# Mixture-of-experts blocks whose weighted results are added to each token's row in DRAM by accumulating scatters

## The chip, the cores and the metric

One core of one Trainium2 chip runs the whole program. The metric is the device time of one execution in microseconds (us), lower is better. Three runs of the kernel before gave 983.85, 988.71 and 992.39 us; their median is 988.71 us. The profile shows one further execution of 982.89 us, whose instructions span 980.9 us.

## What is computed

Four decoder layers work on `x` of 4 x 256 tokens with 256 features (1,024 tokens, eight tiles of 128). Each layer adds a gated attention and a gated feed-forward part to `x`. The change touches the feed-forward parts of layer 0 and layer 3, both mixtures of experts. Layer 0, cut to what matters:

```python
probs = softmax(xf @ gate_w.T)
_, idx = top_k(probs + gate_b, 6)            # 6 of 16 experts per token
cw = weights of the chosen experts, 0 elsewhere    # [tokens, 16]
def expert_step(y, params):
    W1, B1, W2, B2, W3, B3, c = params
    h = silu(xf @ W1.T + B1) * (xf @ W3.T + B3)    # 176 wide
    return y + c[:, None] * (h @ W2.T + B2)
z = shared expert of width 352 with its own biases
x = x + tanh(g_ffn[0]) * (y + z)
```

Layer 3 does the same with 8 experts of width 512, two per token with weights that are divided by their sum, no biases, and a shared expert of width 512. Its result is the program's output.

## The kernel before

**Routing.** `ffn0` and `ffn3` normalise `x` tile by tile. `stored` writes the normalised tokens to a DRAM tensor `xd`, one row of 1 KB per token. The generator `chosen` computes the router's weights `cw`, and `placed` sorts the (token, choice) pairs into blocks of 128 places, each block belonging to one expert: it leaves index columns `gather` and `scatter`, the expert of each block, and `weight`, one number per token and choice. These steps are mostly VectorE instructions; they are handed out one by one between the shared expert's steps `up`, `turn`, `down` (layer 0: L1295 to L1328), which add the shared expert to `x[t]` with `gated_add` (L424).

**Blocks.** `Experts.blocks` (L1225) runs a pipeline over 55 blocks in layer 0 and 20 in layer 3. In step i it gathers the rows of block i+4 (`fetch`, an indirect DMA issued by GpSimd, L1129), transposes block i (`turn`), turns the hidden values of block i-2 (`turn_hidden`), multiplies block i-1 by its expert's first weights (`up`), and block i-2 by the second (`down`). `down` copies the 128 result rows to one of eight places of `ring` and sends them with a second indirect DMA from GpSimd (L1205) to `z`, a DRAM tensor with one row for every (choice, token) pair: 6,144 rows in layer 0, 2,048 in layer 3. No two places share a row, and the scatters are declared independent of each other. Places that hold no token carry an index beyond the end and are skipped. More blocks stand under a condition (L1222) that was false in the profiled run: every engine reads the count and branches past them.

Between layer 0's blocks the generator `fold1` prepares layer 1's weights on TensorE, `ternary1` quantises others on VectorE, and `between` builds 32 diagonal matrices from the weights (L1358).

**Combining.** `combine` (L1241) is called for each of the eight token tiles after all scatters. It loads the tile's rows of `z` with SyncE's queue (L1250; 768 KB per tile in layer 0, in two loads), and adds them with their weights: in layer 0 four of six choices by a matmul with the diagonal matrices into PSUM (L1260), two on VectorE (L1263), and the experts' output biases by a transpose of `cw[:, t, :]` and a matmul with `b2_0` (L1367 to L1370); L1267 then adds PSUM to `x[t]`. In layer 3 both choices go over VectorE. After layer 0, the loads of layer 3's first four experts (L265) wait for the last of these additions, and layer 1's attention starts with `normalised()` on `x` (L354 to L376) and its first matmuls (L389). After layer 3, eight DMAs store `x` (L1619).

Each engine takes its instructions in order. DMAs of one issuing engine are issued in order; SyncE carries all plain loads and stores here, GpSimd all indirect ones.

Of the kernel before, what the change touches and what calls it, by code (L numbers as in the profile page):

```python
# [37 lines left out]
P = 128  # L38
# [19 lines left out]
PEK = 4  # L58
# [18 lines left out]
NOWHERE = 16384.0  # L77
C_SLOTS = 3
FIXED = 2 * DC + 8 + 2 * E0 + E0 + 8 + 2 * E3 + 4 + 1 + NB0 + 8 + 1 + L + 2
FIXED16 = P + K0 * NT + P + E0 * E0  # L80
# [3 lines left out]
def tile_flamingo(ctx: ExitStack, tc: tile.TileContext, a: dict, out: bass.AP):  # L84
# [98 lines left out]
    shared_32 = take(2)[:96]  # L183
    place = take(P, left16)
    tile_of = take(K0 * NT, left16)
# [115 lines left out]
    def prepare():  # L301
# [40 lines left out]
        for rows in (slice(32, 64), slice(64, 96), slice(64, 96)):  # L342

            nc.vector.tensor_tensor(bias_t[rows], bias_t[rows], bias_0[rows], ALU.subtract)
            nc.vector.tensor_copy(bias_0[rows], bias_t[rows])
            yield

# [568 lines left out]
    def chosen(xT, w, n, keep, bias, gate, extra, cut):  # L916
# [45 lines left out]
        nc.vector.tensor_scalar(cw, cw, gate, None, ALU.mult)  # L962
        yield
        return cw, mask

    def placed(cw, mask, n, keep, nb, stride, cut, keeping):
# [66 lines left out]
        for k in range(keep):  # L1033
# [16 lines left out]
                v[:, :, 1, :], is_in, tile_of[:, ts].unsqueeze(2).to_broadcast([P, NT, nb]), ALU.mult  # L1050
# [17 lines left out]
        nc.vector.tensor_scalar(none, row, 0.0, NOWHERE, ALU.is_equal, ALU.mult)  # L1068
# [17 lines left out]
        yield  # L1086
        weight = keeping([P, keep, NT])
        for k in range(keep):
            nc.vector.scalar_tensor_tensor(
                own[:, k, :].rearrange("p (t e) -> p t e", e=n), rank, float(k + 1), cw[:, :, :n], ALU.is_equal, ALU.mult  # L1090
            )
        nc.vector.tensor_reduce(
            weight.rearrange("p k t -> p (k t)"), own.rearrange("p k (t e) -> p (k t) e", e=n), AX.X, ALU.add
        )
        return gather, scatter, expert, offset, weight, used_blocks

    def finish_of(gen, out):

        out.append((yield from gen))

    def stored(normal, name):

        xd = dram.tile([T, D], F32, tag=name, name=name)
        for g, xn in enumerate(normal):
            for i, n in enumerate(xn):
                t = g * TPG + i
                nc.sync.dma_start(out=xd[t * P : (t + 1) * P, :], in_=n)
        return xd

    class Experts:  # L1110


        def __init__(self, route, xd, keep, nb, stride, width, chunk, group, w, bias, hTs, between):
            self.gather, self.scatter, self.expert, self.offset, self.weight, self.used = route
            self.xd, self.keep, self.nb, self.stride = xd, keep, nb, stride
            self.width, self.chunk, self.n = width, chunk, width // chunk
            self.group, self.w, self.bias, self.hTs = group, w, bias, hTs
            self.z = dram.tile([keep * T, D], F32, tag=f"z{group}", name=f"z{group}")
            self.between = between
            self.ring = [sb.tile([P, 4, D], F32, tag="xT", name="ring", bufs=2) for _ in range(2)]  # L1120
            self.scatters: list = []
# [4 lines left out]
        def fetch(self, b):  # L1126

            xs = sb.tile([P, D], F32, tag="xn", name="xs", bufs=6)
# [8 lines left out]
        def turn(self, b):  # L1137
# [4 lines left out]
            del self.xs[b]  # L1142
            nc.vector.tensor_copy(st[:, :D], ps[:, :D])  # L1143
            self.st[b] = st
# [4 lines left out]
        def up(self, b):  # L1149
# [28 lines left out]
            nc.vector.tensor_tensor(s, lin, s, ALU.mult)  # L1178
# [10 lines left out]
        def down(self, b):  # L1189
# [13 lines left out]
            else:  # L1203
                nc.scalar.copy(y, ps[:, :D])
            s = nc.gpsimd.indirect_dma_start(  # L1205
                out=self.z,
# [3 lines left out]
                bounds_check=self.keep * T - 1,  # L1210
                oob_is_err=False,
            )
            if self.scatters:
                tc.declare_no_dep(s.ins, group=self.group, reason="no two places share a row")
            tc.add_to_no_dep_group(self.group, s.ins)
            self.scatters.append(s)
# [24 lines left out]
        def combine(self, t, chunk, diag, more=None):  # L1241


            rows = self.z.rearrange("(k t p) d -> t p k d", t=NT, p=P)
            ps = ps_mm()[:, :D]
            started = more(ps) if more else False
            ends = max(diag, default=-1)
            for lo in range(0, self.keep, chunk):
                zt = t4([P, chunk, D], "zt")
                ld = nc.sync.dma_start(out=zt, in_=rows[t][:, lo : lo + chunk, :])  # L1250
                for s in self.scatters:
                    tc.add_manual_dep(
                        ld.ins,
                        s.ins.name,
                        mybir.DependencyInfo(mybir.DependencyClass.Sync, mybir.DependencyReason.DATA),
                        reason="any place may hold any row",
                    )
                for k in range(lo, lo + chunk):
                    if k in diag:
                        nc.tensor.matmul(ps, diag[k], zt[:, k - lo, :], start=not started, stop=(k == ends))  # L1260
                        started = True
                    else:
                        nc.vector.scalar_tensor_tensor(  # L1263
                            x[t], zt[:, k - lo, :], self.weight[:, k, t : t + 1], x[t], ALU.mult, ALU.add
                        )
# [112 lines left out]
    def ffn3(gate):  # L1378
# [57 lines left out]
        for t in range(NT):  # L1436
            moe.combine(t, K3, {})
# [317 lines left out]
```

## Time and profile before

| what | value |
|---|---|
| median of three runs | 988.71 us |
| profiled execution, its span | 982.89 us, 980.9 us |
| TensorE busy, its mean clock | 872.9 us (89%), 0.939 |
| VectorE, ScalarE, GpSimd busy | 531.6, 274.3, 300.0 us |
| layer 0: first gather, first and last scatter issued | 268.57, 282.32, 446.72 us |
| layer 0: first and last load of `z` | 452.12 us; all 16 issued over 19.4 us |
| layer 3: first and last scatter issued | 857.21, 963.87 us |
| layer 3: loads of `z` begin, stores of `x` begin | 966.46, 971.59 us |
| gather, scatter on GpSimd, each | about 0.97 and 1.02 us |

The columns of a timeline line are start, duration, engine, source line, operation, what it writes and reads, count, and in brackets the idle time of the engine before it with the engine that ended it. A `q` behind an engine's name means its sequencer, as for DMAs that it issues. An indirect DMA's duration on GpSimd is that of its issue; its data land later. Only waits on the engine that is late cost time, so the stages have to be read one by one.

### The profile page before, as it was taken

The numbers are of one execution on the slowest core, as the hardware profiler recorded it, in microseconds if no ns is written. First come the engines' busy times: TensorE is split into PE (matmuls) and PEld (weight loads), VectorE is DVE, ScalarE is ACT, GpSimd is POOL, SyncE is SP. The second block draws the span as 40 slices with busy tenths as digits, with TensorE's granted clock in tenths as the row PEclk, the third lists the DMA queues.
The fourth block names the chain that finished last, engine by engine and source line by source line (L and its number), as shares of the span: only waits on it lengthen the run. The fifth ranks groups of instructions, "written<-read, shape, count | busy, mean of one in ns | idle before, by whom it ended". The sixth has DMA issues, their size and how long they took to land.

```text
span 980.9 us, 12657 instructions
## 1 busy us (share of the span) xinstructions
PE 872.9 (89%) x4451; PEld 569.9 (58%) x4453; DVE 531.6 (54%) x1185; ACT 274.3 (28%) x531; POOL 300.0 (31%) x259
## 2 busy tenths in 40 slices
PE   5999998999899999997899978979638899999992
PEld 3544335876678866774547854746424556666661
DVE  4656455756953344552627749958785855222213
ACT  2211013334123232331223447034303532122220
POOL 1445451310065665751003128003101402133220
PEclk9999999999989999997999999979858989999997
DMA  9200017300154444225730000530000011011004
GB/s 351 84 15 11 28 36 230 89 22 22 33 153 160 131 152 151 90 69 157 260 115 1 1 1 27 189 116 2 22 0 1 1 44 33 22 48 39 29 16 140
DMA packets 35481, 75.82 MB, mean 77 GB/s; under 512 B 4551, under 2 KB 22207, under 8 KB 34106
## 3 DMA queue, kind: packets, MB, share of 16 engines
q1 hardware_dynamic: 27834, 56.22, 17.1%
q0 software_dynamic: 7296, 18.50, 6.1%
q8 instruction: 39, 0.64, 0.3%
q10 hardware_dynamic: 288, 0.26, 0.1%
q14 instruction: 24, 0.20, 0.1%
HBM read 63.42 MB, written 12.98 MB: 78 GB/s over the span
## 4 chain that ended last, share of the span: by engine, by line
PE 53%; DVE 17%; issue 14%; DMA 8%; POOL 4%; ACT 4%; SPq 0%; POOLq 0%; DVEq 0%; ACTq 0%
PE wide L389 9%; PE wide L1158 5%; PE mm L624 5%; DMA zz<-ring,scratch 4%; PE mm L1193 3%; PE wide L1400 3%; PE mm L419 2%; PE mm L1532 2%; POOL zz L1205 2%; PE mm L389 2%; PE wide L609 2%; PE mm L685 1%; PE mm L1421 1%; PE mm L897 1%; PE mm L671 1%
## 5 line engine op out<-in xcount | busy, mean ns | idle before, releaser
L405 POOL TENSOR_TENSOR attn<-attn,sm 128x1024 f32<-128x1024 f32 x32 | 60.8, 1900 | 235.1 <-DVE sm L404 163.1
L1178 DVE TENSOR_TENSOR blk<-wide,blk 128x176 f32<-128x176 f32 (+1 forms) x75 | 32.5, 433 | 142.0 <-ACT blk L1177 142.0
L650 DVE TENSOR_TENSOR rope<-wide,big 128x512 f32<-128x512 f32 x96 | 59.6, 683 | 57.1 <-PE wide L389 55.6
L389 PE MATMUL wide<-xT,big 128*128 128x512 f32 x192 | 88.8, 610 | 0.3 <-ACT big L524 0.3
L1129 POOL DMA_INDIRECT xs<-xd,big x55 | 55.3, 1005 | 70.3 <-DVE shared L1310 34.5
L1158 PE MATMUL wide<-big,blk 128*128 x220 | 74.1, 458 | 0.0
L1169 PE MATMUL wide<-big,blk 128*128 x160 | 72.2, 593 | 0.5 <-DVE blk L1143 0.5
L1205 POOL DMA_INDIRECT zz<-ring,big x55 | 56.1, 1021 | 31.9 <-DVE ring L1202 11.2
L389 PEld LDWEIGHTS wide<-xT,big 128*128 128x128 f32 x192 | 35.7, 193 | 48.7 <-issue 38.7
L1177 ACT ACTIVATE blk<-wide 128x176 f32<-128x176 f32 (+1 forms) x75 | 29.4, 392 | 122.8 <-PE wide L1158 61.6
L624 PE MATMUL mm<-vo,attnT 128*128 128x256 f32 x256 | 60.4, 390 | 0.9 <-ACT attnT L420 0.9
L1193 PE MATMUL mm<-big,blk 88*128 x220 | 56.8, 379 | 0.5 <-ACT blk L1186 0.5
L624 PEld LDWEIGHTS mm<-vo,attnT 128*128 128x128 f32 x256 | 48.4, 194 | 9.5 <-ACT attnT L420 3.3
L420 ACT COPY attnT<-mm 128x512 f32<-128x512 f32 x64 | 35.0, 588 | 65.0 <-PE mm L419 65.0
L374 PE MATMUL mm<-ident,xn 128*128 128x128 f32 x112 | 24.3, 363 | 30.3 <-DVE xn L362 18.0
L1193 PEld LDWEIGHTS mm<-big,blk 88*128 88x128 f32 x220 | 41.4, 189 | 15.5 <-ACT blk L1186 1.4
L1158 PEld LDWEIGHTS wide<-big,blk 128*128 128x128 f32 x220 | 39.5, 190 | 12.5
L403 DVE TENSOR_REDUCE sm<-attn 128x16 f32<-128x1024 f32 x32 | 38.9, 1215 | 14.5 <-ACT attn L397 12.3
L419 PE MATMUL mm<-ident,attn 128*128 128x128 f32 x256 | 36.3, 289 | 10.8 <-POOL attn L405 10.8
L1169 PEld LDWEIGHTS wide<-big,blk 128*128 128x128 f32 x160 | 28.8, 190 | 28.9 <-issue 28.2
L424 DVE SCALAR_TENSOR_TENSOR x<-mm,tg,x 128x256 f32<-128x256 f32 x48 | 22.9, 476 | 39.8 <-PE mm L624 19.7
L1129 POOL DMA_INDIRECT xs<-xd,scratch x20 | 19.2, 961 | 81.5 <-PE mm L1141 59.5
(334 smaller groups left out, 1702.4 us busy)
## 6 DMA issues: line engine op xcount, KB each, us to landing
big<-in_L_w_gate_up SPq DMA_DIRECT2D x8, 1024.0 KB, 8.2
zt<-zz SPq DMA_DIRECT2D x16, 384.0 KB, 5.1
big<-in_L_w SPq DMA_DIRECT2D x4, 1408.0 KB, 6.8
big<-in_L_w_down SPq DMA_DIRECT2D x8, 512.0 KB, 11.9
w_L_qk<-in_L_qk SPq DMA_DIRECT2D x4, 896.0 KB, 8.6
big<-in_L_w SPq DMA_DIRECT2D x4, 704.0 KB
big<-in_L_wo SPq DMA_DIRECT2D x1, 2048.0 KB, 12.8
xd<-xn SPq DMA_DIRECT2D x16, 128.0 KB, 1.8
```

Source lines behind the costliest of these rows:

```text
L389: nc.tensor.matmul(ps, w(c), xT[:, c, :], start=(c == 0), stop=(c == 1))
L403: nc.vector.tensor_reduce(sm, e, AX.X, ALU.add)
L405: nc.gpsimd.tensor_tensor(e, e, sm.unsqueeze(2).to_broadcast([P, groups, n]), ALU.mult)
L419: nc.tensor.transpose(ps[:, i * P : (i + 1) * P], ev[:, pr * P : (pr + 1) * P], ident)
L420: nc.scalar.copy(aT[:, half * 4 : half * 4 + 4, :].rearrange("p i t -> p (i t)"), ps)
L624: nc.tensor.matmul(ps[:, :D], aT[:, s, :], vo[:, s, :], start=(s == 0), stop=(s == NP - 1))
L650: nc.vector.tensor_tensor(m[:, s, :].rearrange("q (b t) -> q b t", t=S), ps[:, s, :].rearrange("q (b t) -> q b t", t=S), table, ALU.mult,)
L1129: nc.gpsimd.indirect_dma_start(out=xs, out_offset=None, in_=self.xd, in_offset=bass.IndirectOffsetOnAxis(ap=self.gather[:, b : b + 1].bitc ...
L1158: nc.tensor.matmul(ps[:, 0, : 2 * n], st[:, c * P : (c + 1) * P], self.w[:, bass.ds(r + c * 2 * n, 2 * n)], start=False, stop=(c == 1),)
L1169: nc.tensor.matmul(ps[:, k, :n], st[:, c * P : (c + 1) * P], self.w[:, bass.ds(r + (2 * c + k) * n, n)], start=(c == 0), stop=(c == 1),)
L1193: nc.tensor.matmul(ps[:, :D], hT[:, j * P : (j + 1) * P], self.w[: self.chunk, bass.ds(r + j * D, D)], start=(j == 0), stop=(j == self.n - 1),
L1205: s = nc.gpsimd.indirect_dma_start(out=self.z, out_offset=bass.IndirectOffsetOnAxis(ap=self.scatter[:, b : b + 1].bitcast(U32), axis=0), i ...
```

## The change

Each block's hidden values are multiplied by the token's weight, which now travels with the token: `xd` rows get 16 (layer 3: 8) more columns with all weights of the token, and each block picks its expert's column. The results are added by the scatter itself (`compute_op=ALU.add`) to the token's own row of a DRAM tensor, `sums0` in two copies for layer 0 (blocks alternate), `sums3` in one for layer 3. The first copy is filled with `x` after the shared expert (`keep_rows`), the second with zeros early in the program. Unused places add to spare rows. `combine`, `z`, the diagonal matrices and `weight` go. The scatters are no longer declared independent, so those that write the same tensor wait for each other. After layer 0 the first copy is loaded into `x` and the second added; after layer 3 `sums3` is copied to the output by DMA. The matmul with the output biases moves into the shared expert's `down`.

```diff
+    spare = take(1)
...
+        zeros = t4([P, 1024], "zeros")
+        nc.gpsimd.memset(zeros, 0.0)
+        for half in range(2):
+            zeroed(sums0[1][half * TH : (half + 1) * TH], zeros)
+        for sums in (*sums0, *sums3):
+            zeroed(sums[T:], zeros)
+        yield
+    sums0 = [dram.tile([T + P, D], F32, tag=f"sums0{i}", name=f"sums0{i}") for i in range(2)]
+    sums3 = [dram.tile([T + P, D], F32, tag="sums3", name="sums3")]
+    def zeroed(rows, zeros):
+        nc.sync.dma_start(out=rows.rearrange("(p r) d -> p (r d)", p=P), in_=zeros[:, : rows.shape[0] * D // P])
+    def keep_rows(sums):
+        for t in range(NT):
+            nc.sync.dma_start(out=sums[t * P : (t + 1) * P, :], in_=x[t])
...
-        weight = keeping([P, keep, NT])
-        for k in range(keep):
-            nc.vector.scalar_tensor_tensor(
-                own[:, k, :].rearrange("p (t e) -> p t e", e=n), rank, float(k + 1), cw[:, :, :n], ALU.is_equal, ALU.mult
-            )
-        nc.vector.tensor_reduce(
-            weight.rearrange("p k t -> p (k t)"), own.rearrange("p k (t e) -> p (k t) e", e=n), AX.X, ALU.add
-        )
...
-        xd = dram.tile([T, D], F32, tag=name, name=name)
+        xd = dram.tile([T, D + n], F32, tag=name, name=name)
...
+    def with_weights(xd, gated):
+        nc.sync.dma_start(out=xd[:, D:].rearrange("(t p) e -> p t e", p=P), in_=gated)
@@ Experts.turn(b)
+            n = self.experts
+            own = small([P, E0], "own")
+            w = self.weight[b] = small([P, 1], "weight", 4)
+            nc.vector.scalar_tensor_tensor(
+                own[:, :n],
+                block[:, :n],
+                self.expert[:, b : b + 1],
+                self.xs.pop(b)[:, D:],
+                ALU.is_equal,
+                ALU.mult,
+                accum_out=w,
+            )
...
-            nc.vector.tensor_tensor(s, lin, s, ALU.mult)
+            nc.vector.scalar_tensor_tensor(s, lin, self.weight.pop(b), s, ALU.mult, ALU.mult)
...
-            s = nc.gpsimd.indirect_dma_start(
-                out=self.z,
+            nc.gpsimd.indirect_dma_start(
+                out=self.sums[b % len(self.sums)],
                 out_offset=bass.IndirectOffsetOnAxis(ap=self.scatter[:, b : b + 1].bitcast(U32), axis=0),
                 in_=y,
                 in_offset=None,
-                bounds_check=self.keep * T - 1,
-                oob_is_err=False,
+                compute_op=ALU.add,
             )
-            if self.scatters:
-                tc.declare_no_dep(s.ins, group=self.group, reason="no two places share a row")
@@ ffn0, down(t)
+            pt = ps_mm()
+            nc.tensor.transpose(pt[:X0, :P], route[0][:, t, :], ident)
+            cwT = sb.tile([P, D], F32, tag="xn", name="cwT", bufs=6)[:X0, :P]
+            nc.scalar.copy(cwT, pt[:X0, :P])
+            nc.tensor.matmul(ps[:, :D], cwT, b2_0, start=False, stop=True)
             gated_add(t, ps[:, :D], gate)
@@ ffn0
+        keep_rows(sums0[0])
...
-            if 8 <= i < 8 + PEK * NT:
-                k, t = divmod(i - 8, NT)
-                nc.vector.tensor_scalar(diags[:, k, t, :], ident, placing[4][:, k, t : t + 1], None, ALU.mult)
...
-            done = moe.combine(t, 3, {k: diags[:, k, t, :] for k in range(PEK)}, bias)
+            nc.sync.dma_start(out=x[t], in_=sums0[0][t * P : (t + 1) * P, :])
+            if t % 2 == 0:
+                more = t4([P, 2, D], "more")
+                nc.scalar.dma_start(
+                    out=more, in_=sums0[1][t * P : (t + 2) * P, :].rearrange("(t p) d -> p t d", t=2)
+                )
+            done = nc.vector.tensor_tensor(x[t], x[t], more[:, t % 2, :], ALU.add)
@@ ffn3
+        keep_rows(sums3[0])
...
-        for t in range(NT):
-            moe.combine(t, K3, {})
...
-    for t in range(NT):
-        nc.sync.dma_start(out=out[t * P : (t + 1) * P, :], in_=x[t])
+    for i in range(4):
+        rows = slice(i * T // 4, (i + 1) * T // 4)
+        engine = nc.scalar if i % 2 else nc.sync
+        engine.dma_start(out=out[rows], in_=sums3[0][rows])
```

## The prediction

> **What bounds the kernel now.** The page's first part says TensorE, its fourth where a chain leaves TensorE:
>
> ```profile
> PE 872.9 (89%) x4451; PEld 569.9 (58%) x4453; DVE 531.6 (54%) x1185; ACT 274.3 (28%) x531; POOL 300.0 (31%) x259
> PE 53%; DVE 17%; issue 14%; DMA 8%; POOL 4%; ACT 4%; SPq 0%; POOLq 0%; DVEq 0%; ACTq 0%
> ```
>
> TensorE's 89% is a mean. The change acts at four places, so I read those: layer 0's hand-over to layer 1, the program's end, the blocks, the shared expert. First the hand-over, in the timeline:
>
> ```profile
> 446.72 0.98 POOL L1205 DMA_INDIRECT zz<-ring,big  x1 [0.94 <-ACT ring L1204]
> ...
> 452.12 19.40 SPq L1250 DMA_DIRECT2D zt<-zz  x16
> ...
> 479.35 0.41 DVE L1267 TENSOR_TENSOR x<-mm,x 128x256 f32<-128x256 f32 x1
> ...
> 481.80 1.92 PE L389 MATMUL mm<-xT,weff 128*128 128x512 f32 x2
> ```
>
> From the last scatter to layer 1's first matmul pass 35.1 us. Utilisation by stretches shows what fills them (columns: us, busy us of PE, PEld, DVE, ACT, POOL with counts, clock, DMA share, GB/s):
>
> ```profile
> 449.00:450.00 1.00, 0.00 (x0) 0.00 (x0) 0.00 (x0) 0.00 (x0) 0.00 (x0) 0.50 0.00 0
> ...
> 455.00:457.00 2.00, 1.66 (x5) 0.64 (x5) 0.00 (x0) 0.25 (x1) 0.00 (x0) 0.50 1.08 347
> ...
> 464.00:470.00 6.00, 5.99 (x26) 4.44 (x27) 4.54 (x14) 0.84 (x3) 0.00 (x0) 1.00 0.92 266
> 470.00:476.00 6.00, 6.00 (x28) 4.28 (x27) 5.38 (x17) 1.50 (x3) 0.59 (x1) 1.00 0.81 266
> ```
>
> At 449 nothing runs; then 6.3 MB of z come in, with TensorE full from 464. Line 1222, the branch past the conditional blocks, explains 449:
>
> ```profile
> L1222 POOLq INC_SWDGE_SEM  x2: 1087/1737/2387, 449.4 to 961.2; - x2
> ```
>
> GpSimd adjusts semaphores for the skipped DMAs; in layer 0 from 449.4 for 2.39 us, and SyncE's load follows. The end, in the chain of waits:
>
> ```profile
> 963.87 2.44 DMA zz<-ring,scratch
> ...
> 967.47 5.09 DMA zt<-zz
> ...
> 974.02 3.26 DVE x L1263 x8
> ```
>
> From the last scatter to the span's end 17.0 us. In the blocks GpSimd's timeline matters, as scatters stay there:
>
> ```profile
> 405.95 0.97 POOL L1129 DMA_INDIRECT xs<-xd,big  x1 [0.34 <-PE mm L1184]
> 407.23 1.02 POOL L1205 DMA_INDIRECT zz<-ring,big  x1 [0.31 <-issue]
> 408.59 0.97 POOL L1129 DMA_INDIRECT xs<-xd,big  x1 [0.34 <-PE mm L1184]
> ```
>
> A block takes 2.64 us here. GpSimd needs 0.97 + 0.30 + 1.02 + 0.30 = 2.6: busy half the time, but without slack where gathers still run.
>
> **What the Trainium skill says.** "DMA: Bandwidth & Descriptors", section Anatomy of one DMA: 2.0 us + bytes/436e3 per us for a DMA from GpSimd, so 2.3 us for 128 KB; the trace has 2.44 us from issue to release, and agrees. The same page, Rules for kernel authors: an accumulating DMA reads its destination and writes it later, so another access to the same bytes has to wait for its semaphore; and accumulation is issued from GpSimd only. "Collectives: The Full Stack", Stop 4, calls such a sum read-read-write with the add free in between. "Perfetto Trace Analysis", DMA Instruction — SWDGE: the recorded end is that of descriptor generation, not of the data; the trace agrees (0.98 against 2.44). No accumulating DMA is in this trace.
>
> **The two unknowns.** *L*, from issue to landing of an adding scatter. Lower bound 2.4 us, the plain one (nothing makes the extra read faster). Estimate from the first page: another 128 KB read, 0.3 us, and one minimal HBM round trip, 0.8 us (section Latency): L = 3.5. Upper bound: no row shows one; plain indirect DMAs beside weight loads land as late as 6 to 7 us after issue by the trace's semaphore events, so I keep 8. *d*, what GpSimd's issue of 1.02 us grows by: 0 if descriptors only carry a flag, 1.0 if the work doubles. I take 0.3.
>
> **The change part by part**, against the execution of 982.9 us (span 980.9 and 2.0 around it; the median is 5.8 higher).
>
> *Layer 0's hand-over.* Last scatter at 446.7, landed at 450.2, GpSimd's 2.4 us and gaps 0.3: loads issue at about 453.0 (before: 452.1). They bring 8 x 128 KB on SyncE and 4 x 256 KB on ScalarE's queue, 2.1 MB instead of 6.3. At the 347 GB/s seen above: 6.0 us plus 2.4 us latency. Half, which the first four tiles need, is in at 458.4, all at 461.4. An addition takes 0.42 us. From the last addition to a transposed group takes 4.6 us before (479.76 to about 484.4, lines 354 to 376). Layer 1's first matmul: 458.4 + 0.4 + 4.6 = 463.4 instead of 481.8, so -18.4. The second group, ready by 466.5, is hidden behind 6.9 us of the first group's matmuls. TensorE starts cold: the clock was 0.50 over the gap and rose at about 463 after eleven us of combining, which is gone; but before it also fell again (0.59 in 481 to 485). I take +0.5, between -1 and 3. Removed with it: 64 matmuls of L1260 (0.41), 16 additions of L1263; they are inside the 35.1 us and not counted twice.
>
> *Program's end.* `sums3` is one chain: scatter 20 waits for scatter 19, issued at 960.65, landed at 964.15: 0.3 late. It lands at 967.7. Two copies per queue, 1 MB read and written: 2.4 + 1 MB at 300 GB/s, 3.5 = 5.9 us, and 1.4 us from last landing to span's end: 975.1. If GpSimd's semaphore work now follows that landing, 1.1 to 2.4 more; half weight, +0.9: 976. So -5, between -8 and -1.
>
> *Shared expert of layer 0.* Eight transposes (0.32), copies (0.25 on ScalarE, beside), eight bias matmuls of two passes (2 x 0.27 at full clock): 0.86 x 8 = 6.9 us of TensorE. Until 269 VectorE bounds this stage with routing (10.00 of 10 us busy in 250 to 270) and hides half; four `down`s run back to back from 269.4 to 275.9, where 3.4 us are on the path. VectorE loses there, ahead of L424, six of L1089 (0.28) and L1092 (0.94): 2.6 us. Net +0.8, between -2 and 4.
>
> *Blocks.* VectorE gains one 128x16 instruction, some 0.2 us (the 128x63 rows take 0.2), and loses 32 x 0.22 of L1358; its multiplication (L1178, 0.34) waits 65.3 us in total for ScalarE, so nothing, at most 1. Its weighted form I price by L1263 against L1267, 0.47 to 0.42 at 128x256: 0.04 more, in the same idle time. The wait: within one copy, scatters of layer 0 are 6.1 us apart on average (164.4 us / 54 x 2), 5.3 in the tail, in layer 3 5.8; L = 3.5 fits. What queues behind a waiting scatter is the next gather, needed four blocks later, then TensorE's transpose; lead 4 x 2.64 - 2.8 = 7.8 us. With d = 0.3, 17 tail blocks fall behind by 5 us, inside the lead: 0. SyncE: eight `keep_rows` issues of 0.36 us from 276.4, behind L1_qk0's load, land at about 283; the first scatter (282.3) waits 0 to 1.5 us, hidden by the lead; `fold1`'s wait for that load may grow, +0.5.
>
> *The rest.* Weights to `xd`: one DMA of 64-byte runs issued at about 238, gathers at 268: hidden. Wider gathers, 6%: 0. Zeros: one GpSimd memset and five stores from some 80 us on, on idle queues; a sixth t4 buffer is gone for about 8 us: 0 to 1. Layer 3's `keep_rows` land by 848, before the scatter at 857: 0.
>
> Sum: -18.4 + 0.5 - 5 + 0.8 + 0.5 + 0.3 = -21.3: 961.6 for this execution, 967 against the median; the execution shown is on the low side of four, so **966**. Its own range: 952 to 977.
>
> **Rivals.** (a) *The add chain becomes the bound: slower.* If L exceeds the spacing, scatters pace GpSimd, the eight ring places fill, and TensorE waits: 27 x (L - 6.1) + 19 x (L - 5.8) us. It eats the gain at L = 6.4; L = 7 costs 47 us: 1013; L = 8: 1060. For it: late landings beside loads; against: a median landing near 2.46. Chance 0.12. (b) *GpSimd's issue grows.* 55 x (2.6 + d) must fit in 171 us plus the lead of 7.8: free to d = 0.65; at d = 1 19 us are lost: 986. For: the 2.6 us above; against: half of the 55 blocks run beside fold steps, with slack. Chance 0.11. (c) *The combine was mostly latency.* Copies DRAM to DRAM at half rate, a cold TensorE, semaphore work behind the last scatter: -10, 978. Chance 0.12. That the adds don't happen is excluded by the code; should both copies be chained as one (spacing 3.04), L = 3.5 costs 25 us: counted in (b).
>
> **How the numbers follow.** The main case has 0.65. Faster by over 1% (below 978.8; about what this kernel's measurement can tell): nearly all of it, half of (c), a third of (b): 0.77; within 1%: 0.12; slower: (a) less a little, and (b)'s end, 0.11. The range 948 to 986 reaches over (c) and most of (b); left out are (a) and the edges, under 0.2.
>
> **What would show it.** Right: loads of `x` near 453, L389 near 463; the end within 12 us of the last scatter; GpSimd waiting little before L1205's successor; scatters still 2.6 us apart in the tail. Wrong: scatters at a constant spacing of L/2 with long idle before them (a); issue near 2 us (b); TensorE idle after 463 (c).

## The result, and the profile after

Five runs of the changed kernel gave a median of 975.17 us (973.77 to 984.07) beside 987.7 us before: ratio 0.9883, 95% interval 0.9849 to 0.9917. The same kernel measured again with the first experiments gave 979.8 us (20 runs) beside 982.86 us (23 runs): 0.9964, interval 0.9942 to 0.9986. The gain is real and small, 12.5 us in the one group and 3 us in the other. The kernel before had medians of 981.5 to 988.3 us on the chips used, so times are compared only within one group of runs. Within a group the time goes with the mean clock that TensorE was granted: in the repetition the fastest run took 971.63 us at 0.940 of full speed, the slowest 985.07 us at 0.931. The profiled execution of the changed kernel took 984.07 us (span 982.3), the slowest of its five.

The table puts the stages side by side, each as one execution of each kernel showed it. "After, again" is the profile of the repetition. "Issued" means that GpSimd's instruction starts; the data land later.

| stage, us | before | after | after, again |
|---|---|---|---|
| layer 0's first scatter issued | 282.3 | 286.9 | 287.9 |
| its first to its last scatter | 164.4 | 176.7 | 176.7 |
| last scatter to layer 1's first matmul | 35.1 | 22.3 | 21.5 |
| from there to layer 3's first scatter (not edited) | 375.4 | 376.7 | 369.9 |
| layer 3's first to last scatter | 106.7 | 109.3 | 109.3 |
| last scatter to the span's end | 17.0 | 10.5 | 10.0 |
| span | 980.9 | 982.3 | 975.3 |

The edited stages add up to +0.2 and -0.1 us: what the hand-over and the end gave was taken back in front of them. The stretch that no edit touches moves by several us from one execution to the next, so single spans prove little here, and the stages show more. On the page of the changed kernel, three rows answer to those of before: busy time by engine, the software queue's packets, MB and share, and the scatter's group (total and mean ns of one, idle before it):

```profile
PE 860.7 (88%) x4389; PEld 557.0 (57%) x4389; DVE 527.7 (54%) x1261; ACT 274.0 (28%) x531; POOL 343.7 (35%) x260
...
q0 software_dynamic: 14496, 20.47, 12.8%
...
L1225 POOL DMA_INDIRECT sums<-ring,big x55 | 87.8, 1596 | 32.1 <-issue 15.7
```

GpSimd issues an adding scatter in 1.596 us, a plain one in 1.021 before. The queue's packets doubled (7,296 before) and their share too (6.1% before), with 18.5 MB grown to 20.5 only. The trace's DMA records show where they come from: an adding scatter moves its 128 KB in 128 packets of 1 KB, one for each row, a plain one (the plain scatters of the experiments below) in 32 packets of 4 KB. From issue to landing, by the semaphore events of the trace, an adding scatter takes 3.8 us in the median (a plain one 2.45), but those issued at 297.2, 326.9, 363.6 and 384.9 us, within 1 us of weight loads that SyncE issues, take 6.5 to 9.65 us. The timeline at the hand-over of layer 0:

```profile
463.54 1.55 POOL L1225 DMA_INDIRECT sums<-ring,big  x1 [0.63 <-issue]
469.14 5.50 SPq L1355 DMA_DIRECT2D x<-sums  x8
...
476.23 0.43 DVE L1361 TENSOR_TENSOR x<-x,more 128x256 f32<-128x256 f32 x1 [1.04 <-DMA x<-sums]
...
480.23 0.30 ACT L375 ACTIVATE rstd<-mv,eps 128x4 f32<-128x4 f32 x1 [7.25 <-DVE mv L373]
...
482.22 3.81 PE L392 MATMUL mm<-ident,xn 128*128 128x128 f32 x16 [25.56 <-DVE xn L380]
485.82 14.64 PE L407 MATMUL mm<-xT,weff 128*128 128x512 f32 x31
```

The loads start 5.6 us after the last scatter, and layer 1's first matmul follows 16.7 us after them. At the end of the program:

```profile
966.10 1.55 POOL L1225 DMA_INDIRECT sums<-ring,scratch  x1 [4.17 <-ACT ring L1224]
...
971.80 1.55 POOL L1225 DMA_INDIRECT sums<-ring,scratch  x1 [4.15 <-DMA sums<-ring,scratch]
975.70 1.21 SPq L1609 DMA_DIRECT2D out_dram<-sums  x2
```

The last scatter waits for the landing of the one before it; the copies to the output start 3.9 us after it is issued.

### The profile page after: what moved, and what is told of

It reads as the page before. It is cut to its first block, busy times and chain, and to the rows that moved or that the text cites. A ratio compares the mean times of both kernels' runs of the same rounds, so it can differ in the third digit from the quotient of the medians.

```text
span 982.3 us, 12516 instructions
## 1 busy us (share of the span) xinstructions
PE 860.7 (88%) x4389; PEld 557.0 (57%) x4389; DVE 527.7 (54%) x1261; ACT 274.0 (28%) x531; POOL 343.7 (35%) x260
## 3 DMA queue, kind: packets, MB, share of 16 engines
q0 software_dynamic: 14496, 20.47, 12.8%
## 4 chain that ended last, share of the span: by engine, by line
PE 34%; DVE 11%; ACT 3%; POOL 1%; issue 1%; DMA 1%; POOLq 0%; ACTq 0%; DVEq 0%
PE wide L1189 7%; PE mm L407 5%; PE mm L1213 3%; PE wide L1389 3%; PE mm L642 2%; PE mm L1520 2%; PE mm L437 2%; PE mm L915 1%; PE mm L1410 1%; PE mm L392 1%; DVE mx L884 1%; DVE big L1436 1%; PE wide L873 1%; DVE attn L886 1%; DVE sm L421 1%; DVE big L1437 1%
## 5 line engine op out<-in xcount | busy, mean ns | idle before, releaser
L1198 DVE SCALAR_TENSOR_TENSOR blk<-wide,weight,blk 128x176 f32<-128x176 f32 (+1 forms) x75 | 37.0, 493 | 133.6 <-ACT blk L1197 130.7
L1225 POOL DMA_INDIRECT sums<-ring,big x55 | 87.8, 1596 | 32.1 <-issue 15.7
L1178 PE MATMUL wide<-big,blk 128*128 x220 | 76.5, 469 | 0.0
L1189 PE MATMUL wide<-big,blk 128*128 x160 | 72.2, 593 | 0.5 <-DVE blk L1150 0.5
L392 PEld LDWEIGHTS mm<-ident,xn 128*128 128x128 f32 x112 | 18.2, 189 | 62.3 <-ACT rstd L375 31.7
L1213 PEld LDWEIGHTS mm<-big,blk 88*128 88x128 f32 x220 | 41.9, 192 | 16.7 <-ACT blk L1206 1.5
L1178 PEld LDWEIGHTS wide<-big,blk 128*128 128x128 f32 x220 | 40.3, 194 | 12.9 <-issue 0.8
L437 PE MATMUL mm<-ident,attn 128*128 128x128 f32 x256 | 36.9, 292 | 11.5 <-POOL attn L423 11.5
L1137 POOL DMA_INDIRECT xs<-xd,scratch x20 | 19.4, 972 | 76.9 <-PE mm L1149 51.9
```

What stands on the lines that cost most here:

```text
L392: nc.tensor.transpose(ps[:, i * P : (i + 1) * P], n[:, c * P : (c + 1) * P], ident)
L437: nc.tensor.transpose(ps[:, i * P : (i + 1) * P], ev[:, pr * P : (pr + 1) * P], ident)
L1137: nc.gpsimd.indirect_dma_start(out=xs, out_offset=None, in_=self.xd, in_offset=bass.IndirectOffsetOnAxis(ap=self.gather[:, b : b + 1].bitc ...
L1178: nc.tensor.matmul(ps[:, 0, : 2 * n], st[:, c * P : (c + 1) * P], self.w[:, bass.ds(r + c * 2 * n, 2 * n)], start=False, stop=(c == 1),)
L1189: nc.tensor.matmul(ps[:, k, :n], st[:, c * P : (c + 1) * P], self.w[:, bass.ds(r + (2 * c + k) * n, n)], start=(c == 0), stop=(c == 1),)
L1213: nc.tensor.matmul(ps[:, :D], hT[:, j * P : (j + 1) * P], self.w[: self.chunk, bass.ds(r + j * D, D)], start=(j == 0), stop=(j == self.n - 1),
```

## Experiments

All were run beside the kernel before. Two theories on the 12 us that the blocks of layer 0 lost: the **chain** (a scatter waits for an earlier one to the same copy, and some land late) or **GpSimd's issue** (0.57 us more per scatter, 55 times).

### The changed kernel again

> The changed kernel once more, as the base of its group: its one profiled execution took 984 us, its other four runs about 975 us. If the 9 us are that execution's alone, this one's profile spans about 973 us, with GpSimd's scatters at 1.59 us and 3.19 us apart where gathers still run, and with the last scatter of layer 0 about 177 us after the first in either case.

Measured: 979.8 us, 0.9964; its stages are in the table above and repeat those of the first profile within 1.1 us, the unedited stretch apart.

### Plain scatters, four copies, one copy

The kernel with plain scatters leaves the addition out, the one with four copies never adds the last two to `x`.

```diff
@@ plain scatters
-                compute_op=ALU.add,
@@ four copies
-    sums0 = [dram.tile([T + P, D], F32, tag=f"sums0{i}", name=f"sums0{i}") for i in range(2)]
+    sums0 = [dram.tile([T + P, D], F32, tag=f"sums0{i}", name=f"sums0{i}") for i in range(4)]
@@ one copy
-        moe = Experts(placing, xd, E0, NB0, W0, F0, FC0, sums0, big[:, : E0 * W0], (bias_0, choice), hTs, between)
+        moe = Experts(placing, xd, E0, NB0, W0, F0, FC0, sums0[:1], big[:, : E0 * W0], (bias_0, choice), hTs, between)
```

> Scatters write without adding (the sums keep the last write alone), all waits and all other work kept. Issue theory (GpSimd's longer instruction paces layer 0's blocks): issue back to 1.02 us, scatters 2.65 us apart in the tail, 165 us from first to last instead of 177, so 10 to 14 us faster than the changed kernel. Chain theory (each scatter waits for the landing of the one before on its copy): faster too, by a similar amount, as landing falls from 3.8 to 2.5 us; the four copies tell the two apart. Hand-over theory (nothing is lost in the blocks, all of it after the last scatter): no more than 2 us.

> Layer 0's scatters go to four copies instead of two (the third and fourth are zeroed but not added to x), so a scatter waits for the one four blocks earlier; issue cost unchanged. Issue theory: scatters stay 3.19 us apart where gathers run, only the last ones, without gathers, close up from 2.2 to 1.9 us: 1 to 3 us faster than the changed kernel. Chain theory: as fast as the plain scatters, 10 us or more.

> Layer 0's scatters all go to one copy, so that each waits for the landing of the one before; the second copy stays zero and is still added, so the work after the blocks is the same. With a landing of 3.8 us and 0.3 us to restart, scatters come 4.1 to 4.2 us apart: 54 x 4.15 = 224 us from first to last instead of 177, so 45 to 50 us slower. If the chain were free (landing overlapped with GpSimd's issue), no change.

| kernel | us, ratio (interval) | issue, us | first to last scatter, layer 0 | layer 3 | end |
|---|---|---|---|---|---|
| changed, again | 979.8, 0.9964 (0.9942 to 0.9986) | 1.60 | 176.7 | 109.3 | 10.0 |
| plain scatters | 963.99, 0.9801 (0.9763 to 0.9839) | 1.00 | 165.2 | 106.7 | 8.8 |
| four copies | 970.35, 0.9862 (0.9811 to 0.9913) | 1.59 | 165.2 | 109.2 | 11.5 |
| one copy | 1062.23, 1.0808 (1.0764 to 1.0853) | 1.59 | 264.4 | 109.3 | 10.3 |

Four copies have the slow issue and no waits for landings, and their blocks are as fast as those of plain scatters: the chain costs the 12 us. Plain scatters keep the chain, but land sooner; they wait for landings too (11 times, 5.9 us) and lose nothing by it. No run has the adding scatter's landings together with the plain one's issue, so whether the chain would cost as much without the slower issue is not shown. The dependencies' view of the scatters (GpSimd's idle time ahead of them, us and times, by what ended it) shows the chain for the changed kernel

```profile
  ACT ring L1224: 22.1, 6
  issue: 19.0, 43
  DVE ring L1222: 16.2, 4
  DMA sums<-ring,big: 5.4, 4
```

and for four copies no row "DMA sums<-ring,big" is left in that view, while one copy has this one:

```profile
  DMA sums<-ring,big: 43.8, 15
```

Only 5.4 us are put down to the chain in the changed kernel, though it lost 11.5 us against four copies. The time of single scatters, counted from each kernel's first, shows where:

| block | 6 | 21 | 30 | 45 | 54 |
|---|---|---|---|---|---|
| before | 19.4 | 68.1 | 96.4 | 142.4 | 164.4 |
| changed | 22.6 | 72.2 | 106.8 | 156.8 | 176.7 |
| four copies | 20.3 | 69.2 | 98.1 | 147.9 | 165.2 |

The changed kernel falls behind in jumps, not evenly. Its timeline at two of them:

```profile
307.57 1.58 POOL L1225 DMA_INDIRECT sums<-ring,big  x1 [2.60 <-DMA sums<-ring,big]
...
393.63 1.58 POOL L1225 DMA_INDIRECT sums<-ring,big  x1 [3.88 <-issue]
```

The first of them waits for the scatter issued at 297.16, the last one before it to the same copy, which took 9.65 us to land. The second is put down to "issue", but it too starts 0.76 us after such a landing: the scatter issued at 384.94 took 7.93 us. The view infers what ended a wait, and it misses some. By the semaphore events, ten of the 55 scatters start 0.72 to 0.79 us after the landing of the last one to the same copy, and GpSimd's idle time ahead of these ten, less the usual 0.30 us each, adds up to 12.2 us. With four copies no scatter waits so. Behind a waiting scatter stands the next gather: VectorE's first instruction on the gathered rows (L1155) waits for them nine times in layer 0, 11.7 us in all, and never with four copies. Later the blocks run at GpSimd's own pace:

```profile
434.10 1.59 POOL L1225 DMA_INDIRECT sums<-ring,big  x1 [0.30 <-issue]
435.99 0.98 POOL L1137 DMA_INDIRECT xs<-xd,big  x1 [0.30 <-PE wide L1178]
```

1.59 + 0.30 + 0.98 + 0.30 = 3.2 us a block, 2.64 before. With four copies this alone puts GpSimd 5.5 us behind the kernel before at block 45, inside the gathers' lead, and the last blocks, which have no gathers, catch up to 0.8. With two copies the jumps come first (8.7 us behind four copies at block 30), nothing in a 3.2 us cycle can make them up, and TensorE waits: its last `down` ends at 456.7 instead of 451.0, and GpSimd's last scatter follows 6.9 us later instead of 0.7.

One copy gives the chain's price: 264.4 us for 54 gaps, 4.90 us each, 4.6 in the median; that is the landing of 3.8 us and some 0.7 until the next is issued, plus late landings. It cost 82 us against the changed kernel, more than expected: the expectation had 0.3 us until the next is issued, and the late landings all count there. Plain scatters and four copies differ by 4.9 us in their spans (962.3 and 967.2), all of it in layer 3, which still has one copy: 2.5 us in its scatters, the rest at the end.

### Additions on GpSimd, loads on two queues

```diff
@@ both
-            done = nc.vector.tensor_tensor(x[t], x[t], more[:, t % 2, :], ALU.add)
+            engine = nc.vector if t < TPG else nc.gpsimd
+            done = engine.tensor_tensor(x[t], x[t], more[:, t % 2, :], ALU.add)
@@ loads on two queues
-            nc.sync.dma_start(out=x[t], in_=sums0[0][t * P : (t + 1) * P, :])
+            (nc.sync, nc.scalar)[t % 2].dma_start(out=x[t], in_=sums0[0][t * P : (t + 1) * P, :])
```

> The additions of the second group's four tiles (L1361, t = 4 to 7) go from VectorE to GpSimd, which is idle there; loads unchanged. Theory 'VectorE's order': in the changed kernel the first group's statistics end at 480.2 because additions of tiles 4 to 7 wait for their loads ahead of them on VectorE; the fourth tile of the first group had landed by about 476.2. Then the first rstd (L375) should start some 2 to 3 us earlier after the loads' issue (8.5 to 9 us instead of 11.1), and layer 1's first matmul 14 us after the loads' issue instead of 16.7; time lower by 2 to 3 us, about 0.997 of the changed kernel's. Rival 'loads': the loads themselves are late, the first rstd moves by under 1 us and the time stays. Rival 'cold clock': the transposes start earlier but TensorE is granted less, and the gain is lost by the attention's first matmuls.

> As the kernel before it, and the eight loads of x alternate between SyncE's and ScalarE's queue, where they were all on SyncE's, issued over 5.5 us. Theory 'issue': the fourth tile of the first group is issued about 2 us earlier and lands as much earlier, so the first rstd starts at 6.5 to 7.5 us after the loads' issue and layer 1's first matmul at 12 to 13 us. Rival 'bandwidth': all loads of a stretch share the same DMA engines, landings don't move, and it equals the kernel before it within 1 us.

Measured: 978.08 us, 0.9933 (0.9899 to 0.9966), and 979.13 us, 0.9974 (0.9959 to 0.9989). The first rstd (the end of the first group's statistics; a group is four tiles) came 9.4 and 9.1 us after the loads' issue (11.1 and 10.3 in the two profiles of the changed kernel), the first matmul 15.5 and 15.4 us after (16.7 and 15.9). The additions were 1 to 2 us of the wait for rstd, and at most 1.3 us of that for the matmul, as VectorE had other work of the second group left in front; a second queue moved nothing: its loads landed 2.5 to 5.5 us after issue all the same. Neither total can be told from the changed kernel's.

### Bias transposes first

```diff
@@ ffn0, down(t)
+            pt = ps_mm()
+            nc.tensor.transpose(pt[:X0, :P], route[0][:, t, :], ident)
+            cwT = sb.tile([P, D], F32, tag="xn", name="cwT", bufs=6)[:X0, :P]
+            nc.scalar.copy(cwT, pt[:X0, :P])
             hT = held.pop(t)[:FC0, 512:]
...
-            pt = ps_mm()
-            nc.tensor.transpose(pt[:X0, :P], route[0][:, t, :], ident)
-            cwT = sb.tile([P, D], F32, tag="xn", name="cwT", bufs=6)[:X0, :P]
-            nc.scalar.copy(cwT, pt[:X0, :P])
             nc.tensor.matmul(ps[:, :D], cwT, b2_0, start=False, stop=True)
```

> In the shared expert's down of layer 0 the transpose of the weights and ScalarE's copy (L1318, L1320) stand ahead of the four matmuls instead of behind them; the same instructions. Theory 'wait': the 4 to 4.5 us by which the first scatter comes later (286.9 against 282.3) are TensorE's waits for ScalarE's copy between transpose and bias matmul; then the first scatter comes 2 to 3 us earlier, 284 to 285, and the time is lower by as much. Rival 'work and clock': it is the added TensorE work (24 passes at a clock of 0.5 to 0.6), which stays: first scatter at 286 to 287, time unchanged.

Measured: 971.0 us, 0.9886 (0.9848 to 0.9924). The first scatter came at 282.6 instead of 286.9, more than expected, and nothing was given back: the last came at 459.2 instead of 463.5. In this pair of profiles the order of the same instructions was worth 4.3 us, over all twelve with layer 0 changed some 3: the first scatter comes at 286.0 us in the mean of the nine with the bias behind the matmuls (283.6 to 287.9), at 283.2 in the mean of the three with it first (282.6 to 283.9). TensorE's timeline at the end of the shared expert, changed kernel:

```profile
275.51 0.27 PE L1318 MATMUL mm<-ident,cw 128*18 128x128 f32 x1
276.18 0.89 PE L1321 MATMUL mm<-b,cwT 18*128 18x256 f32 x2 [0.40 <-ACT cwT L1320]
277.01 1.06 PE L1174 MATMUL wide<-bias,big 96*128 96x352 bf16 x2
```

and with the transposes first (lines 1311 and 1320 are transpose and bias matmul there):

```profile
272.92 0.28 PE L1311 MATMUL mm<-ident,cw 128*18 128x128 f32 x1
273.04 1.89 PE L1317 MATMUL mm<-w_L_s,shared 88*128 88x256 f32 x8
274.86 0.69 PE L1320 MATMUL mm<-b,cwT 18*128 18x256 f32 x2
275.49 0.66 PE L1149 MATMUL mm<-ident,xs 128*128 128x128 f32 x4
```

The waits go, and TensorE is done with the shared expert 1.5 us earlier in this pair; over all profiles that end lies at 273.2 to 277.6 us in the nine and at 275.6 to 276.5 in the three, so that explains nothing. What differs comes behind it: from TensorE's last bias matmul to the first scatter pass 9.8 to 10.6 us in the nine and 6.4 to 7.8 in the three. There the clock differs too. Utilisation by stretches (the clock is the third column from the right), changed kernel and transposes first:

```profile
276.00:279.00 3.00, 2.46 (x6) 0.79 (x6) 0.63 (x3) 0.13 (x1) 1.28 (x2) 0.59 0.89 229
279.00:282.00 3.00, 2.86 (x6) 1.70 (x7) 1.30 (x8) 0.00 (x0) 2.43 (x3) 0.50 0.96 257
```

```profile
276.00:279.00 3.00, 2.67 (x12) 1.37 (x9) 1.96 (x13) 0.32 (x1) 2.39 (x4) 1.00 0.94 239
279.00:282.00 3.00, 2.25 (x13) 1.37 (x14) 0.78 (x4) 1.06 (x3) 1.91 (x2) 1.00 0.95 275
```

The first blocks ran at half clock in the changed kernel. The nine kernels with the bias behind the matmuls all have such a stretch (0.50 to 0.51 in 279 to 282 us or just before it), the three with the bias first have 1.00 throughout. The kernel before has one too, from 270 to 276, where the shared expert's last matmuls still ran. By the clock's records the nine lie at 0.50 for 3.4 to 6.8 us, which is 1.7 to 3.4 us of work lost, about what they are later. Each of the nine has two waits of 0.3 and 0.4 us for ScalarE's copy here, the three have none. That the short waits bring the fall about is likely by this, but only the order was tried. The time fell by more than this stage explains: 971.0 us beside 979.13 with the loads on two queues, measured in the same group, where the stage gave some 4. The granted clock of whole runs was 0.943 in the median beside 0.933; why it differs by so much is open.

### Three copies

```diff
-        for half in range(2):
-            zeroed(sums0[1][half * TH : (half + 1) * TH], zeros)
+        for copy in sums0[1:]:
+            for half in range(2):
+                zeroed(copy[half * TH : (half + 1) * TH], zeros)
-    sums0 = [dram.tile([T + P, D], F32, tag=f"sums0{i}", name=f"sums0{i}") for i in range(2)]
+    sums0 = [dram.tile([T + P, D], F32, tag=f"sums0{i}", name=f"sums0{i}") for i in range(3)]
...
+                third = t4([P, 2, D], "third")
+                nc.scalar.dma_start(
+                    out=third, in_=sums0[2][t * P : (t + 2) * P, :].rearrange("(t p) d -> p t d", t=2)
+                )
-            done = nc.vector.tensor_tensor(x[t], x[t], more[:, t % 2, :], ALU.add)
+            nc.vector.tensor_tensor(x[t], x[t], more[:, t % 2, :], ALU.add)
+            done = nc.vector.tensor_tensor(x[t], x[t], third[:, t % 2, :], ALU.add)
```

> Three copies of layer 0's sums instead of two: blocks go round, the third is filled with zeros early and loaded and added after the blocks (1 MB more, four DMAs and eight additions). The result is the reference's. Theory 'chain': with three blocks between two adds to one copy (about 9 us at GpSimd's pace) even landings of 7 us are waited for hardly at all: first to last scatter 165 to 166 us instead of 176.7, the last scatter within 2 us of the last down; the hand-over grows by 3 to 4 us for the loads; time lower by 7 to 9 us, 0.991 to 0.993 of the changed kernel's. Rival 'GpSimd's issue': 1.59 us per scatter is the loss, first to last stays over 172 and the time is higher than with two copies by the 3 to 4 us of the loads.

Measured: 969.29 us, 0.9871 (0.9839 to 0.9903). First to last scatter 167.3 us, the last at 450.9; the hand-over took 25.2 us, 3 to 4 more. This is close to what the chain theory had (165 to 166 us), and far from GpSimd's issue (over 172).

### Each layer's half alone

The first has layer 0 with `z` and `combine` as before and layer 3 changed, the second the reverse. The lines are cut to one for each; `ExpertsB` is the class of the kernel before.

```diff
@@ ffn0, layer 3 alone changed
-        moe = Experts(placing, xd, E0, NB0, W0, F0, FC0, sums0, big[:, : E0 * W0], (bias_0, choice), hTs, between)
+        moe = ExpertsB(placing, xd, K0, NB0, W0, F0, FC0, "z0", big[:, : E0 * W0], (bias_0, choice), hTs, between)
@@ ffn3, layer 0 alone changed
-        moe = Experts(route[0], xd, E3, NB3, W3, F3, P, sums3, big, None, hTs, lambda i: None)
+        moe = ExpertsB(route[0], xd, K3, NB3, W3, F3, P, "z3", big, None, hTs, lambda i: None)
+        for t in range(NT):
+            moe.combine(t, K3, {})
```

> Layer 0 as in the kernel before, layer 3 and the program's end as in the changed one. Theory 'stages': by the traces layer 3's scatters take 2.6 us longer (the wait for the landing ahead of the last ones) and the end is 6.5 to 7 us shorter, so about 4 us are gained against the kernel before: 0.996. First to last scatter of layer 0 stays 164.4 us, the hand-over 35 us. Rival 'layer 0 earns it': the end alone is worth nothing that can be told (0.998 to 1.002), as the first stage's gain would have to come from layer 0.

> Layer 0 as in the changed kernel, layer 3 and the program's end as in the one before. Theory 'stages': first scatter 4.5 us later, the blocks 12 us longer, the hand-over 13 us shorter: layer 0's change as a whole loses 3 to 4 us against the kernel before, 1.003 to 1.004. Rival 'layer 0 earns it': 0.990 to 0.997, with the gain outside the three stages (attention and feed-forward parts between, which the edits don't touch).

Measured: layer 3 alone 978.16 us, 0.9961 (0.9945 to 0.9977); layer 0 alone 982.08 us, 0.9997 (0.9981 to 1.0012). Together they give 0.9958, which agrees with the 0.9964 of the whole. The end earns what the change earns; layer 0 earns nothing that can be measured, nor does it lose the 3 to 4 us expected. Its stages: first scatter 285.2, blocks 176.3, hand-over 21.6 us.

### All mends, and the order after the hand-over

The first joins three copies, bias first, two queues and GpSimd's additions, which are issued from `late()` in `normalised` behind the first group's tiles. The second puts the additions back on VectorE and adds two orders: the second group's additions behind the first group's last normalised tile, and its transposes behind the first group's last matmul.

```diff
@@ all mends
+            if g == 1:
+                late()
@@ first group first, on top of it
-            engine = nc.vector if t < TPG else nc.gpsimd
+            if t >= TPG:
+                tc.add_manual_dep(
+                    first.ins,
+                    kept["normal"].ins.name,
...
+            xT = transposed(layernorm(g), after=last)
```

> All mends together on the changed kernel: three copies of the sums in layer 0, the bias transpose ahead of the shared expert's matmuls, the loads after layer 0 on two queues, additions of the second group on GpSimd and behind the first group's normalisation in the order. The result is the reference's. If the mends add up: three copies give 5 us (measured alone), the bias first 4 to 5, the additions and queues 1 to 2: 11 us below the changed kernel on this chip, about 967 to 968 where the kernel before takes 981, ratio 0.984 to 0.988. Rival: they overlap (an earlier first scatter only lets GpSimd fall behind sooner), and it gains no more than the best of them alone, 0.987 to 0.989.

> As the kernel with all mends, but the second group's additions are back on VectorE, with an order that puts them behind the first group's normalised tiles, and TensorE's transposes of the second group stand behind the first group's matmuls. The result is the reference's. Theory 'order': with all mends the first rstd came 11.8 us after the loads' issue, the reciprocal of the first group another 4.2 us later behind the second group's statistics, and TensorE transposed both groups ahead of its first matmul: first matmul 20.2 us after the loads' issue. In this order nothing of the second group stands in front: first matmul 14 to 15 us after the loads' issue, hand-over 20 us instead of 25.8, time 3 to 5 us lower, 963 to 965. Rival 'second group': TensorE then waits for the second group's xT after the first group's 16 matmuls, which take some 7 us, and half or more of it is given back: 966 to 968.

All mends: 968.12 us, 0.9871 (0.9849 to 0.9893). That is the ratio of three copies alone; it lies in the expectation's range and in its rival's, and the mends do not add up. The first scatter came at 283.0, the blocks took 166.3 us, but the hand-over 25.8. Its timeline has the reason:

```profile
466.66 0.30 ACT L376 ACTIVATE rstd<-mv,eps 128x4 f32<-128x4 f32 x1 [2.12 <-DVE mv L374]
...
469.64 0.43 DVE L373 BATCH_NORM_STATS2 st<-x 128x6 f32<-128x256 f32 x1 [1.53 <-POOL x L1374]
...
470.88 0.14 DVE L377 RECIPROCAL rstd<-rstd 128x4 f32<-128x4 f32 x1
...
471.68 3.56 PE L393 MATMUL mm<-ident,xn 128*128 128x128 f32 x16 [23.07 <-DVE xn L381]
475.08 2.31 PE L410 MATMUL mm<-xT,weff 128*128 128x512 f32 x5
```

The first group's rstd is done at 467.0; the reciprocal behind it on VectorE stands 3.9 us later, behind statistics of the second group that wait for GpSimd's additions (0.7 us each, on VectorE 0.4). Then TensorE transposes both groups before the first matmul. With the order mended:

```profile
466.89 0.30 ACT L376 ACTIVATE rstd<-mv,eps 128x4 f32<-128x4 f32 x1 [1.15 <-DVE mv L374]
467.22 0.18 DVE L377 RECIPROCAL rstd<-rstd 128x4 f32<-128x4 f32 x1 [0.36 <-ACT rstd L376]
...
468.05 2.10 PE L393 MATMUL mm<-ident,xn 128*128 128x128 f32 x8 [18.73 <-DVE xn L381]
...
470.18 15.11 PE L415 MATMUL mm<-xT,weff 128*128 128x512 f32 x30
```

The first matmul comes 14.6 us after the loads and the hand-over takes 20.2 us, as expected; the time is 966.19 us, 0.9769 (0.974 to 0.9798), in the rival's range. But the rival's reason is not there: the first group's matmuls took over 15 us, not some 7, and TensorE did not wait for the second group. From the last scatter to layer 3's first pass 396.5 us, with all mends 397.5: of 5.6 us only 1.0 stays in the profiles. By the timeline TensorE pays some 2 us with its clock and some 1 with the second group's transposes, which now come later; the remainder is within what the stretch behind moves from one execution to the next. The stretch just after its start, by the utilisation view:

```profile
470.10:475.00 4.90, 4.87 (x8) 2.21 (x8) 3.95 (x15) 0.81 (x3) 0.00 (x0) 0.58 0.32 89
```

That is eight matmuls at a clock of 0.58, where TensorE does 13 in the five us after it, at a clock of 1.00. In the kernel with all mends the same slow stretch fell on the transposes (0.51 in 470 to 475). By the clock's records, counted from the last scatter, full clock came 25.6 us behind it with all mends and 24.2 with the mended order, though TensorE's work began at 22.4 and 18.1. The ratio is better by 1% than that of all mends, the time by 1.9 us; they were measured on two chips, on which the kernel before takes 988.3 and 982.8 us, and how much of the 1% is the chip's stays open. Both are faster than the kernel before and, by their times, than the changed one.

## Why the prediction was right, and where it was not

The measured 975.2 lies in the range around 966, 948 to 986, and faster by over 1% was the likeliest outcome; the first group has it (1.2%), the repetition has 0.4%. The sum behind it did not hold: the edited places were to give 21.3 us and gave none in the two traces.

- **Right: GpSimd's issue is free to d = 0.65.** d, what its issue grows by, was 0.57, near that limit and above the 0.3 taken; the blocks with four copies and with plain scatters both take 165.2 us. Rival (b) did not happen.
- **Nearly right: L = 3.5.** The median time to landing is 3.8. Its upper bound of 8 was passed once in the profile (9.65).
- **The step that failed: "L = 3.5 fits", in Blocks.** It compared the mean spacing within a copy, 6.1 us, with one typical landing, and then counted the lead of 7.8 us as cover for GpSimd's lag. Landings beside weight loads passed the spacing several times, each with a jump, and the 0.7 us from a landing to the next issue was not in it. The lead was already used for 5.5 us by the slower issue, which also left no slack to catch up (3.2 of every 3.2 us taken); that both were needed is argued from the times, not tried. Predicted 0, measured +12 us. This is rival (a)'s mechanism with late landings in the place of a high median; its formula, with L = 3.8, gives nothing.
- **Mis-sized: the shared expert, +0.8.** It was +4.5 to +5.6 in the two profiles. Added TensorE work was counted, the copy between transpose and bias matmul was put "beside" on ScalarE, and the clock was not considered; the order alone took some 3 us of it away (4.3 in the pair shown).
- **Mis-sized: the hand-over, -18.4 + 0.5.** It was -12.8 and -13.6. The loads came 5.6 us after the last scatter, close to the 6.3 taken; from there 16.7 us in place of 10.4. The loads of the first group landed 7 us after the first issue in place of 5.4; VectorE had the second group's work in front of the first's; and TensorE transposed both groups first, 3.8 us, half of it for the second. The last is partly only moved: the kernel before has the second group's transposes after its first matmul.
- **Right: the end, -5.** It was -6.5 and -7.0 (copies landed 3.5 to 4.85 us after issue, 5.9 taken), less 2.6 for the last scatters of layer 3, where the chain was taken as 0.3 late. Together -4, and layer 3 alone measured -3.8 (0.9961).
- **Right: what was hidden.** Zeros, the weights' store and layer 3's `keep_rows` landed before anyone waited; VectorE's weight per block (0.31 us) ended one wait of TensorE, 0.3 us long.

So the direction was right for one of the reasons, the end's. That the time fell into the range was luck: the hand-over gave 5 us less than was summed, two terms put at 0 and 0.8 took some 17, and the stages came to about 0. The halves and the whole, measured later, agree on some 4 us. The first group's 12.5 us are not explained by the stages; the changed kernel's runs had a clock of 0.939 in the median there and 0.935 in the repetition, which goes with 975.2 beside 979.8, and the rest is open.

## What to carry to other kernels

A chain of dependent transfers is judged by its late landings, not by its typical one: ask how the engine that issues them catches up after one, and if its cycle has no slack, give the chain another copy before anything else (three in place of two took off 9 us of 12, for 3 to 4 us of loads). A small dependent piece on TensorE goes ahead of the work that can cover its copy, since short waits may cost clock beyond their own length, which is likely here and not shown. After a wait that all engines share, look at each engine's order of instructions for work of the second group that stands in front of the first.

## What was not expected of the hardware

- An adding scatter of 128 rows of 1 KB costs GpSimd 1.60 us of issue in place of 1.02 and moves in 128 packets of 1 KB in place of 32 of 4 KB; it lands after 3.8 us in the median (2.45), beside weight loads after up to 9.65.
- Dependent adding scatters to one tensor follow each other at 4.4 us at best, 4.6 in the median and 4.9 in the mean; from a landing to the next issue pass 0.72 to 0.79 us.
- TensorE's clock fell to 0.50 for 3.4 to 6.8 us behind a stage with waits of 0.3 to 0.4 us in nine kernels, and stayed at 1.00 in all three where the same instructions ran in another order, without these waits.
- TensorE began its work after a pause 4.3 us earlier and had its full clock 1.4 us earlier: of 5.6 us gained at the hand-over, 1.0 was left.
